# Layer 1 of a two-layer network: results, amplitudes, results, and the angles of an image further ahead

## The chip, the cores and the metric

The kernel runs on one NeuronCore of a Trainium2 chip. The metric is the device time of one execution in microseconds (us). The kernel before took 1475.18 us in the median of three runs (1472.35 to 1476.03).

## The reference

The input x has 16 images of 128 channels and 64 by 64 pixels, in float32. Two layers follow each other, and each adds its result to its input.

Layer 0 normalises x over groups of four channels and runs a diagonal LSTM over it: 127 sequential steps, each with a product of the gate weights and the states of the step before. Layer 1 treats every pixel on its own. It is this part that the change touches:

```python
xq = xf @ pre_w.T + pre_b            # 128 channels -> 4 angles a pixel
z = _simulate(xq, q_weights)         # 4 qubits, 16 complex amplitudes, 4 expectations
out = z @ post_w.T + post_b          # 4 -> 128 channels
x = x + out                          # xf is the group-normalised x
```

`_simulate` is linear in products of the sines and cosines of the angles, so the kernel writes it as sine of sums of angles, a fixed matrix that gives the amplitudes, their squares, and a matrix that leads from the squares to the 128 output channels.

## The kernel before

Layer 0 runs as one long loop of steps over all images at once, with its result kept in the on-chip buffer `ring`, which holds 40 of the 64 rows of every image. The lower 24 rows are written to a scratch tensor `low` in device memory, and layer 1 loads them back. Statistics of layer 0's result close that part, and `b_image` (L730) is the last value that layer 1 waits for.

Layer 1 then goes image by image. An image is 4096 pixels, taken as eight tiles of 128 channels by 512 pixels: tiles 0 to 2 come from `low`, tiles 3 to 7 lie in `ring`. For image b there are these stages:

- `load(b)`: three DMAs of 256 KB on GpSimd's queue (POOL, L749) fetch tiles 0 to 2 into buffers of the pool `lowp`.
- `angles(b)`: eight matmuls (16 passes in the profile, L760) write the angles of all pixels of the image into one PSUM tile `theta`. The same function then makes the sines: ScalarE adds the image's bias (L770), VectorE takes off the nearest whole turn with two instructions (L771, L772), ScalarE takes the sine (L773). The result `y` is kept in `turns`.
- `squares(b)`: two matmuls (L780) give the amplitudes `am`, and ScalarE squares each (L782) into a tile `sq`.
- `outputs(b, h)` for the halves h = 0 and 1: four matmuls (L789) give four PSUM tiles `po`, 512 pixels each.
- `finish(b, h, po)`: VectorE adds each `po`, the output bias and the input tile in place (L806). SyncE's queue (SP) writes the result out: in half 0 the three low tiles of 256 KB each (L808) and one piece of `ring` of 256 KB, in half 1 one piece of 1 MB (both L811).

All of this stands under a hand-written order (`manual_schedule`): each engine runs its instructions in the order in which the source issues them. Before the loop come the loads of images 0 to 2, `angles(0)`, `angles(1)` and `squares(0)`. Round b of the loop is then: `load(b+3)`, `outputs(b,0)`, `finish(b,0)`, `angles(b+2)`, `outputs(b,1)`, `squares(b+1)`, `finish(b,1)`.

The pool `lowp` has 11 buffers, two more than the nine of three images. A load into a buffer waits until the result of the tile that was in it has been written out. So in round b the first two tiles of image b+3 take buffers of image b-1, and its third takes the buffer of tile 0 of image b, whose writing out is issued in that same round. The tiles `po` have one buffer each, so that `outputs(b,1)` follows the evictions of `finish(b,0)` tile by tile. The pool `trp` holds two buffers each of `y` and of the two `sq`.

Of the kernel before, what the change touches and what calls it, by code (L numbers as in the profile page):

```python
# [11 lines left out]
F32 = mybir.dt.float32  # L12
# [4 lines left out]
P = 128  # L17
NB = 16
# [8 lines left out]
CHUNK = 2 * BLOCK  # L27
# [51 lines left out]
def kernel(  # L79
# [50 lines left out]
    def block(r):  # L130

        return (r + AHEAD if r < SLOTS else r - SLOTS) // ROWS
# [600 lines left out]

    lowp = ctx.enter_context(tc.tile_pool(name="lowp", bufs=11))
    trp = ctx.enter_context(tc.tile_pool(name="trp", bufs=2))
    ps_t = ctx.enter_context(tc.tile_pool(name="ps_t", bufs=2, space=PSUM))
    ps_a = ctx.enter_context(tc.tile_pool(name="ps_a", bufs=1, space=PSUM))
    ps_o = ctx.enter_context(tc.tile_pool(name="ps_o", bufs=1, space=PSUM))  # L740
    NT = NLOW * NW // CHUNK
    x1s, turns, sqs = {}, {}, {}

    def load(b):

        x1s[b] = []
        for k in range(NT):
            lt = lowp.tile([P, CHUNK], F32, name=f"low{b}_{k}", tag="low")
            nc.gpsimd.dma_start(out=lt, in_=low[b, :, k * CHUNK : (k + 1) * CHUNK])  # L749
            x1s[b].append(lt)  # L750
        for r in range(NLOW, NH, 2 * ROWS):
            q = block(r)
            x1s[b].append(ring[:, q : q + 2, b, :])

    def angles(b):
        th = ps_t.tile([P, CHUNK], F32, name=f"theta{b}", tag="theta")
        for h in range(2):

            for j in (2, 3, 1, 0):
                nc.tensor.matmul(  # L760
                    th[32 * j : 32 * j + 32, :],
                    lhsT=w_image[:, b, 16 - 16 * h : 48 - 16 * h],
                    rhs=x1s[b][2 * j + h],
                    start=(h == 0),
                    stop=(h == 1),
                    tile_position=(0, 32 * j),
                )

        y = trp.tile([P, CHUNK], F32, name=f"y{b}", tag="y")
        nc.scalar.activation(y, th, AF.Identity, bias=b_image[:, b : b + 1])  # L770
        nc.vector.tensor_scalar(th, y, ROUND, ROUND, ALU.add, ALU.subtract)  # L771
        nc.vector.tensor_sub(y, y, th)  # L772
        nc.scalar.activation(y, y, AF.Sin, scale=TWO_PI)  # L773
        turns[b] = y

    def squares(b):
        sqs[b] = []
        for h in range(2):
            am = ps_a.tile([P, CHUNK], F32, name=f"am{b}_{h}", tag=f"am{h}")
            nc.tensor.matmul(am, lhsT=w_amp[:, h, :], rhs=turns[b], start=True, stop=True)  # L780
            s = trp.tile([P, CHUNK], F32, name=f"sq{b}_{h}", tag=f"sq{h}")
            nc.scalar.activation(s, am, AF.Square)  # L782
            sqs[b].append(s)

    def outputs(b, h):
        po = [ps_o.tile([P, CHUNK], F32, name=f"po{b}_{h}_{j}", tag=f"po{j}") for j in range(4)]
        for j in range(4):
            k = 32 * j
            nc.tensor.matmul(  # L789
                po[j],  # L790
                lhsT=w_out[k : k + 32, :],
                rhs=sqs[b][h][k : k + 32, :],
                start=True,
                stop=True,
                tile_position=(k, 0),
            )
        return po

    def finish(b, h, po):
        for j in range(4):  # L800
            k = 4 * h + j
            x1 = x1s[b][k]
            y = po[j]
            if k >= NT:
                y = y.rearrange("p (k n) -> p k n", n=BLOCK)
            nc.vector.scalar_tensor_tensor(x1, y, b_out, x1, ALU.add, ALU.add)  # L806
            if k < NT:
                nc.sync.dma_start(out=ov[b, :, k * CHUNK : (k + 1) * CHUNK], in_=x1)  # L808
        for r0, r1 in (((NLOW, SLOTS),), ((SLOTS, NH),))[h]:
            q = block(r0)  # L810
            nc.sync.dma_start(  # L811
                out=ov[b, :, r0 * NW : r1 * NW].rearrange("c (k n) -> c k n", n=BLOCK),
                in_=ring[:, q : q + (r1 - r0) // ROWS, b, :],
            )

    with tc.manual_schedule():
        for b in range(3):
            load(b)
        angles(0)
        angles(1)  # L820
        squares(0)
        for b in range(NB):
            if b + 3 < NB:
                load(b + 3)
            po = outputs(b, 0)
            finish(b, 0, po)
            if b + 2 < NB:
                angles(b + 2)
            po = outputs(b, 1)
            if b + 1 < NB:  # L830
                squares(b + 1)
            finish(b, 1, po)


# [35 lines left out]
```

## Time and profile before

| What | Value |
|---|---|
| median of three runs | 1475.18 us |
| profiled execution, own time | 1472.09 us |
| its span | 1470.3 us |
| layer 1: from b_image (1310.63) to the end of the span | 159.7 us |
| busy in the whole span | PE 1368.3, VectorE 975.4, GpSimd 890.1, ScalarE 765.4 us |
| moved by DMA in the whole span | 106.99 MB |

Times within the profile count from the start of the span. PE is TensorE, DVE is VectorE, ACT is ScalarE, POOL is GpSimd, SP is SyncE. PEclk is the granted clock of TensorE as a share of its full speed. The shares of the whole span are averages over two unlike layers: in layer 0, which is most of the time, TensorE is busy nearly throughout and DMA is nearly idle; in layer 1, the last tenth, DMA is busy nearly throughout.

### The profile page before, as it was taken

To read this page: it belongs to the slowest core of one execution; us is meant where nothing else is said; L and a number is where in the kernel's file an instruction comes from. 1 tells how busy PE (TensorE), PEld (TensorE's weight loads), DVE (VectorE), ACT (ScalarE), POOL (GpSimd) and SP (SyncE) were. 2 spreads that over 40 slices of the span, in tenths; PEclk is the share of its full clock that TensorE was granted. 3 is DMA by queue.
4 is the path that set the end of the run, shared out by engine and by line. 5 is a ranking of instruction groups with operands and counts; after the bars stand their busy time and mean duration, and the time that the engine had idled before them with its cause. 6 is when DMAs were issued, how large, how long until landed. Compare 5 with 4: busy or idle time off the path is not lost. (4 is left out here: it accounts for less than half of the span.)

```text
span 1470.3 us, 19434 instructions
## 1 busy us (share of the span) xinstructions
PE 1368.3 (93%) x5798; PEld 970.2 (66%) x5798; DVE 975.4 (66%) x2458; ACT 765.4 (52%) x1862; POOL 890.1 (61%) x1694
## 2 busy tenths in 40 slices
PE   4658999999999999999999999999999999859987
PEld 3658887777667767676677677767776787832322
DVE  6974566566765667877767775555555678767765
ACT  3545666565555555555555555555555665422221
POOL 1125787766667767788788767666766776521110
PEclk9999999999999999999999999999999999979987
DMA  9970000000000000134433000000000000028987
GB/s 311 375 254 1 2 1 1 1 1 1 1 0 1 1 0 1 58 128 138 135 118 112 1 1 0 1 1 1 0 1 1 1 1 1 1 79 303 327 281 269
DMA packets 86192, 106.99 MB, mean 73 GB/s; under 512 B 4024, under 2 KB 70728, under 8 KB 86088
## 3 DMA queue, kind: packets, MB, share of 16 engines
q1 hardware_dynamic: 80576, 92.29, 18.4%
q0 software_dynamic: 3840, 12.59, 2.7%
q8 instruction: 46, 0.75, 0.2%
q10 hardware_dynamic: 1672, 0.89, 0.2%
q14 instruction: 58, 0.48, 0.1%
HBM read 59.61 MB, written 46.14 MB: 72 GB/s over the span
## 5 line engine op out<-in xcount | busy, mean ns | idle before, releaser
L491 PE MATMUL ps<-xn,wxT 128*128 128x512 f32 (+18 forms) x1280 | 480.7, 518 | 2.0 <-POOL xn L483 2.0
L604 DVE TENSOR_TENSOR ps<-ps,both 128x256 f32<-128x256 f32 (+9 forms) x544 | 219.7, 408 | 325.7 <-PE ps L582 320.2
L608 ACT ACTIVATE ps<-ps,bias 128x512 f32<-128x512 f32 (+23 forms) x480 | 268.5, 581 | 252.5 <-DVE ps L604 213.0
L491 PEld LDWEIGHTS ps<-xn,wxT 128*128 128x128 f32 x1280 | 231.8, 191 | 174.5 <-issue 155.5
L633 ACT COPY both<-ps 128x256 f32<-128x256 f32 (+9 forms) x544 | 191.7, 355 | 178.5 <-PE ps L582 158.9
L582 PE MATMUL ps<-diff,w1T 128*128 128x256 f32 (+14 forms) x1088 | 283.7, 363 | 0.0
L582 PE MATMUL ps<-diff,w0T 128*128 128x256 f32 (+14 forms) x1088 | 283.2, 362 | 0.0
L524 POOL TENSOR_TENSOR ring<-ring,hst 128x256 f32<-128x256 f32 (+8 forms) x488 | 247.5, 539 | 24.7 <-DVE hst L672 24.7
L582 PEld LDWEIGHTS ps<-hst,wsT 128*128 128x128 f32 x1088 | 195.9, 190 | 85.5 <-DVE hst L672 35.4
L582 PE MATMUL ps<-hst,wsT 128*128 128x256 f32 (+14 forms) x1088 | 241.3, 365 | 5.7 <-DVE hst L672 4.3
L582 PEld LDWEIGHTS ps<-diff,w0T 128*128 128x128 f32 x1088 | 199.7, 190 | 21.2
L582 PEld LDWEIGHTS ps<-diff,w1T 128*128 128x128 f32 x1088 | 199.2, 190 | 20.8
L483 POOL TENSOR_TENSOR xn<-xn,rstd 128x512 f32<-128x512 f32 (+10 forms) x160 | 170.7, 1067 | 15.2 <-DVE rstd L152 2.7
L478 POOL TENSOR_TENSOR xn<-ring 128x256 f32<-128x256 f32 (+8 forms) x213 | 147.4, 702 | 0.0
L672 DVE TENSOR_TENSOR hst<-g,ps 128x256 f32<-128x256 f32 (+13 forms) x320 | 108.4, 369 | 44.9 <-ACT g L663 41.7
L663 ACT ACTIVATE g<-cst 128x256 f32<-128x256 f32 (+20 forms) x320 | 103.0, 368 | 64.1 <-DVE cst L662 63.6
L473 POOL TENSOR_TENSOR xn<-ring,mean 128x16 f32<-128x16 f32 (+8 forms) x247 | 130.7, 539 | 3.6 <-DVE mean L138 2.6
L515 POOL TENSOR_TENSOR diff<-hst 128x240 f32<-128x240 f32 (+9 forms) x136 | 103.0, 758 | 39.0 <-DVE hst L672 35.7
L662 DVE TENSOR_TENSOR cst<-cst,ps 128x256 f32<-128x256 f32 (+20 forms) x320 | 104.6, 368 | 5.5
L659 DVE TENSOR_TENSOR ps<-ps,g 128x512 f32<-128x512 f32 (+20 forms) x160 | 95.1, 594 | 18.6 <-ACT g L608 17.6
L685 POOL COPY edge<-hst 128x16 f32<-128x16 f32 x64 | 25.1, 392 | 135.9 <-DVE hst L672 135.9
L652 DVE TENSOR_TENSOR cst<-cst,ps 128x512 f32<-128x512 f32 (+20 forms) x160 | 92.8, 580 | 16.9 <-ACT ps L608 9.4
(149 smaller groups left out, 1219.9 us busy)
## 6 DMA issues: line engine op xcount, KB each, us to landing
ring<-in_x_dram SPq DMA_DIRECT2D x16, 1024.0 KB, 7.5
out_dram<-ring SPq DMA_DIRECT2D x16, 1024.0 KB, 5.9
rest<-in_x_dram SPq DMA_DIRECT2D x48, 256.0 KB, 5.0
low<-ring SPq DMA_DIRECT2D x6, 2048.0 KB, 7.5
ring<-in_x_dram SPq DMA_DIRECT2D x6, 2048.0 KB, 8.4
low<-low POOLq DMA_DIRECT2D x48, 256.0 KB, 4.0
out_dram<-low SPq DMA_DIRECT2D x48, 256.0 KB, 6.1
ring<-in_x_dram SPq DMA_DIRECT2D x16, 256.0 KB, 7.8
```

The source lines that it names most:

```text
L473: nc.gpsimd.tensor_sub(by_pairs(xn, 0, j, n), x0, over(mean1, n))
L478: nc.gpsimd.tensor_sub(by_pairs(xn, 1, j, n), lower, of)
L483: nc.gpsimd.tensor_mul(v, v, r)
L491: nc.tensor.matmul(ps[g][:, :, a:b], lhsT=wxT[:, g * 128 : (g + 1) * 128], rhs=xns[t % 2][:, :, a:b], start=True, stop=True,)
L515: nc.gpsimd.tensor_sub(diff[:, 0, a1:b], now[:, 1, a1 - NB : b - NB], now[:, 0, a1:b])
L524: nc.gpsimd.tensor_add(x1, x1, by_pairs(new, q, j, n))
L582: nc.tensor.matmul(out, lhsT=w[:, g * 128 : (g + 1) * 128], rhs=rhs, start=False, stop=True, skip_group_check=True,)
L604: nc.vector.tensor_add(v, v, both[g][:, a:b])
L608: nc.scalar.activation(to[:, :, a:w], ps[g][:, :, a:w], FUNC[g], bias=bias[:, g : g + 1])
L633: nc.scalar.copy(both[g][:, a:b], ps[g][:, 0, a:b])
L662: nc.vector.tensor_add(c[:, q], c[:, q], ig[:, q])
L672: nc.vector.tensor_mul(new[:, q, a:v], th[:, q, a:v], act[GO][:, q, a:v])
```

## The change

The stages stay the same, with the same matmuls, the same instructions on VectorE and ScalarE and the same DMAs. What changes is their order and their buffers.

`angles` keeps only the matmuls. A new function `sines` holds the four instructions that followed them; it is a generator that stops before the sine, so that the caller can place the two parts apart. Loads run four images ahead (12 buffers), the matmuls of the angles three images ahead at the end of a round, and the sines two images ahead in the middle of it. Round b is now: `load(b+4)`, `outputs(b,0)`, `finish(b,0)`, the first three instructions of `sines(b+2)`, `squares(b+1)`, the sine of image b+2, `outputs(b,1)`, `finish(b,1)`, `angles(b+3)`. Round 0 is an exception: it takes the angles and the sines of image 2 after its results, and then the angles of image 3. The second square is written over `y`, which has three buffers; the first has two.

```diff
-    lowp = ctx.enter_context(tc.tile_pool(name="lowp", bufs=11))
-    trp = ctx.enter_context(tc.tile_pool(name="trp", bufs=2))
+    lowp = ctx.enter_context(tc.tile_pool(name="lowp", bufs=12))
+    sinp = ctx.enter_context(tc.tile_pool(name="sinp", bufs=3))
+    sqp = ctx.enter_context(tc.tile_pool(name="sqp", bufs=2))
...
-
-        y = trp.tile([P, CHUNK], F32, name=f"y{b}", tag="y")
+        ths[b] = th
+
+    def sines(b):
+
+        th = ths[b]
+        y = sinp.tile([P, CHUNK], F32, name=f"y{b}", tag="y")
         nc.scalar.activation(y, th, AF.Identity, bias=b_image[:, b : b + 1])
         nc.vector.tensor_scalar(th, y, ROUND, ROUND, ALU.add, ALU.subtract)
         nc.vector.tensor_sub(y, y, th)
+        turns[b] = y
+        yield
         nc.scalar.activation(y, y, AF.Sin, scale=TWO_PI)
-        turns[b] = y
 
     def squares(b):
-        sqs[b] = []
+        ams = []
         for h in range(2):
             am = ps_a.tile([P, CHUNK], F32, name=f"am{b}_{h}", tag=f"am{h}")
             nc.tensor.matmul(am, lhsT=w_amp[:, h, :], rhs=turns[b], start=True, stop=True)
-            s = trp.tile([P, CHUNK], F32, name=f"sq{b}_{h}", tag=f"sq{h}")
+            ams.append(am)
+
+        sqs[b] = [sqp.tile([P, CHUNK], F32, name=f"sq{b}", tag="sq"), turns[b]]
+        for am, s in zip(ams, sqs[b]):
             nc.scalar.activation(s, am, AF.Square)
-            sqs[b].append(s)
...
     with tc.manual_schedule():
-        for b in range(3):
+        for b in range(4):
             load(b)
         angles(0)
+        for _ in sines(0):
+            pass
         angles(1)
+        later = sines(1)
+        next(later)
         squares(0)
+        next(later, None)
         for b in range(NB):
-            if b + 3 < NB:
-                load(b + 3)
+            if b + 4 < NB:
+                load(b + 4)
             po = outputs(b, 0)
+            later = sines(b + 2) if 0 < b < NB - 2 else iter(())
             finish(b, 0, po)
-            if b + 2 < NB:
-                angles(b + 2)
-            po = outputs(b, 1)
+            next(later, None)
             if b + 1 < NB:
                 squares(b + 1)
+            next(later, None)
+            po = outputs(b, 1)
             finish(b, 1, po)
+            if b == 0:
+                angles(2)
+                for _ in sines(2):
+                    pass
+            if b + 3 < NB:
+                angles(b + 3)
```

More of the change, by code (lines that the diff above doesn't have):

```diff
@@ L741 @@
     NT = NLOW * NW // CHUNK
-    x1s, turns, sqs = {}, {}, {}
+    x1s, ths, turns, sqs = {}, {}, {}, {}
     def load(b):
```

## The prediction, made before the result was known

> **What bounds the kernel now.** I first read the slices of the whole span (40 slices of 36.8 us), to see where layer 1 differs from layer 0.
>
> ```profile
> PE   4658999999999999999999999999999999859987
> DVE  6974566566765667877767775555555678767765
> DMA  9970000000000000134433000000000000028987
> ```
>
> TensorE carries layer 0; in the last four slices DMA comes up to 9. The change touches only those. Next, windows of layer 1; the columns are the window, its length, busy PE, PEld, DVE, ACT and POOL, the granted clock, the DMA share and GB/s.
>
> ```profile
> 1340.00:1360.00 20.00, 18.23 (x88) 5.73 (x92) 13.30 (x20) 4.83 (x9) 3.22 (x6) 1.00 0.97 333
> 1360.00:1380.00 20.00, 18.91 (x84) 5.96 (x76) 15.52 (x24) 5.82 (x11) 3.22 (x6) 1.00 0.96 334
> 1400.00:1420.00 20.00, 15.14 (x65) 4.05 (x63) 9.80 (x16) 3.17 (x5) 3.22 (x6) 0.83 0.77 257
> 1440.00:1471.00 31.00, 22.54 (x72) 7.54 (x72) 18.72 (x29) 3.93 (x7) 0.00 (x0) 0.76 0.72 245
> ```
>
> DMA is nearly full at times (333/0.97 to 334/0.96: about 345 GB/s) and far from it at others. What leaves it idle is in the chain that ended last (start, length, what). This is one turn of it, from image 6 to image 8:
>
> ```profile
> 1373.23 0.71 DVE low L806
> 1373.95 6.74 DMA out_dram<-low
> ...
> 1381.24 3.23 DMA low<-low
> ...
> 1384.51 1.91 PE theta L760 x12
> 1386.42 1.07 PE po L789 x8
> 1387.49 1.07 PE am L780 x2
> ...
> 1388.61 2.50 DVE ring L806 x4
> ...
> 1391.29 0.71 DVE low L806
> ```
>
> A low tile is evicted, written out, its buffer reloaded, and the angles that need the reload hold up the outputs two rounds later. Last, where rounds begin on SP's queue:
>
> ```profile
> 1392.01 3.20 SPq L808 DMA_DIRECT2D out_dram<-low  x3
> ...
> 1400.20 3.00 SPq L808 DMA_DIRECT2D out_dram<-low  x3
> ...
> 1415.75 2.84 SPq L808 DMA_DIRECT2D out_dram<-low  x3
> ...
> 1423.70 2.55 SPq L808 DMA_DIRECT2D out_dram<-low  x3
> ```
>
> A round with its reload in time takes 7.95 us (1415.75 to 1423.70). One with a late reload takes more, once 15.55 us. All round starts: 1323.03, 1329.87, 1337.60 (rounds 0 to 2), 1442.13 (13), 1450.08 (14), 1460.29 (15); end 1470.3. Rounds 2 to 12 average (1442.13 - 1337.60)/11 = 9.50 us.
>
> **What the skill says.** The Trainium skill, page "DMA: Bandwidth & Descriptors", section Specifications, gives about 358 GB/s of device memory per core; my 345 fits. The same page, section "Queues, rings and completion order", says that each DMA engine takes the queues that have work in turn. The trace agrees: in 1340 to 1400 a reload of 256 KB took 2.8 to 7.4 us to land (median 5.1), beside the writing out. Page "TensorE: Matmul & The Clock Gate", section "What's actually happening", says that an idle window of some 3.4 us halves the clock. At 1406.53, after 4.86 us of waiting, a theta pass took 1.07 us and not 0.59, at a clock of 0.50; but the clock also fell at 1432 without such a wait[...]. Page "SBUF — State Buffer", section "Who interferes with whom", has VectorE and GpSimd share a port in some operations. The trace puts most of POOL's reload waits down to VectorE, but VectorE's evictions have one SBUF tensor, so I can't tell a lock from a coincidence; one instruction (0.74 us) bounds it, and the 0.55 us below contains the usual part.
>
> **The change, part by part.** No instruction is added or removed, so each part is a matter of place.
>
> *Angles at the end of a round, sines in its middle.* In a free round of before, VectorE waits 1.27 us for ACT's y, between finish(b,0) and the rounding of image b+2, because theta runs just ahead of it. That theta is now a round old, and the wait goes. What VectorE then has in a round: eight evictions at a pitch of (1422.93 - 1420.30)/4 = 0.66 us, 0.73 for L771 and 0.61 for L772, 6.6 us in all. PE: theta 1.9, am 2.0, po 2 x 1.1, 6.1 us. ACT: 0.69 + 0.63 + 2 x 0.6 = 2.5 us. So engines alone allow about 6.6 us a round instead of 7.95.
>
> *What DMA needs in a round:* 2.10 MB out and 0.79 MB in, 2.88 MB, at 345 GB/s 8.4 us. Engines of 7.95 or 6.6 us both outrun it; DMA or the loop through it decides.
>
> *The loop through the reload.* Before: from the eviction's start 0.77 us to the issue, 6.2 to landing (median in 1340 to 1400, 4.9 to 7.5), 0.55 to POOL's issue (1380.69 to 1381.24), 5.1 to landing, then from theta (1384.51) to the eviction (1391.29) 6.78: 19.4 us for two rounds, 9.7 each. The measured 9.50 confirms the sum. After: all three tiles of image b+4 take the buffers of image b, so the last waits for the third eviction, issued at 2.05 and not 0.77. Then 6.2 + 0.55 + 5.1 as before. But this theta stands ahead of po(b+2,0) and of nothing else: theta 1.91, po 1.14, and the eviction follows. 2.05 + 6.2 + 0.55 + 5.1 + 3.05 = 16.95 us for two rounds, 8.5 each. So the distance costs 1.3 us of a later reload and saves 3.7 us behind it. A late theta now holds po(b+2,0), am and everything behind them on PE; the sines of the image before and its evictions are already queued on VectorE and hide the first part. I take 8.5 us for rounds 2 to 12, since it is the largest of 6.6, 8.4 and 8.5. Bounds: with all landings longest (7.5 and 7.4) 20.55/2 = 10.3; with all shortest the loop gives 6.7, and DMA at 358 GB/s holds it to 8.05.
>
> *The start.* sq of image 0 stood behind the sine of image 1 on ACT and po began at 1321.03. Now it follows am directly: am begins at 1317.86, its first tile is done near 1318.9, sq takes 0.6, po begins near 1319.6: 1.4 us earlier. The 12th load goes out with the first 11, which end near 1306 and hide it; theta starts at 1310.9. Without that cover it would cost up to 3.4 us.
>
> *Rounds 0 and 1.* Round 0 has theta of two images behind po(0,1), before po(1,0): 2 x 1.9 us, of which the four evictions (2.7 us) hide a part. Counted from the first eviction at 1320.75: po(0,1) ends 1323.8, thetas 1327.6, po(1,0) 1328.7, so 7.9 us; before 6.84. Round 1: 7.0 by VectorE's 6.6 and the hand-overs; before 7.73.
>
> *Rounds 13 and 14.* No reload is left. Round 13: VectorE's 6.6 and what DMA has piled up, 7.2 (before 7.95). Round 14: before, am(15) stood behind po(14,1), and VectorE sat idle for 4.85 us waiting for po(15,0). Now am is ahead: 6.0 us at full clock; at half clock, where am took 3.78 and po 2.04, 0.6 + 3.78 + 2.04 + 2.7 = 9.1. I take 8.0 (before 10.21). Last round, unchanged: 10.0.
>
> *The other edits* (squares in place, buffer counts) cost nothing: y is read by both am passes before it is overwritten, three buffers of y cover the two images in work, and the square it feeds is needed a round later, under some 8 us of other work.
>
> Sum: 1321.6 + 7.9 + 7.0 + 11 x 8.5 + 7.2 + 8.0 + 10.0 = 1455.2 us of span, against 1470.3: 15.1 us less. The profiled execution's own time (1472.09) lies 1.8 us above its span, and the median of the runs 3.1 us above that; I take the difference off the median: 1475.2 - 15.1 = 1460.1 us.
>
> **Rivals.** *Reloads still late in part:* landing times lie between 4.9 and 7.5 and between 2.8 and 7.4, and a fuller DMA lengthens them; rounds of 9.1 give 11 x 0.6 = 6.6 us more, 1466.7. For it: the 6.47 us reload at 1400. Against it: the writing out is issued in order, so while a reload is on its way there is work behind it. *The distance is cancelled:* the later third tile eats what was saved, rounds stay at 9.5; the start and the end alone give -1.4 + 1.1 - 0.7 - 0.75 - 2.2 = -4.0, 1471.2. *Slower, by TensorE's clock:* PE's idle time now gathers at one place, ahead of theta. If that leaves the clock at 0.50, a round on PE is theta 3.62, am 3.78, po 2 x 1.8, 11.0 us: 11 x 1.5 = 16.5 more than before, less 4.0, 1487.7. The total is slower than before from 9.5 + 4.0/11 = 9.9 us a round, measurably from 10.3. Against it: 2.3 us of idle time in a round of 8.5 is short of the 4.86 us at 1406; for it: the drop at 1432. *Faster still:* DMA at 8.05 us a round and a full clock at the end, 1460 - 5 - 2 = 1453.
>
> **Chances.** The forecast 0.60, reloads still late 0.20, cancelled 0.10, slower 0.08, faster still 0.02. A change under 0.3% (4.4 us) can't be told from none with this kernel. Faster: 0.60 + 0.20 + 0.02 and a part of the cancelled, 0.84; within 0.3% 0.08; slower 0.08. The range 1453 to 1472 leaves out the slower case and a part of the cancelled one.
>
> **What would show it.** Right: round starts 8.3 to 8.7 us apart from round 2 to 12, none above 11; a DMA share of 0.97 or more there; VectorE's wait for y (39.5 us in all before) nearly gone; first issue on SP near 1321.6; VectorE's 4.85 us gap near the end shorter. Wrong: theta still waiting some us for low in most rounds with DMA share below 0.95 (loop longer than I sum), a clock of 0.5 in the middle of the layer, or a POOL queue that issues its reloads well over 0.6 us after the writing out has landed.

## The result, and the profile after

The changed kernel takes 1465.99 us in the median of 18 runs (1460.61 to 1470.85), the kernel before 1472.99 us in the 18 runs beside them. The ratio is 0.9952 with a 95% interval of 0.9939 to 0.9965: faster by 0.5%, 7.0 us, where 15.1 us were forecast.

The profiled execution of the changed kernel has a span of 1468.0 us. The slices of its whole span (36.7 us each) look like those of before, with layer 1 in the last four:

```profile
PE   4658999999999999999999999999999999858987
DVE  6883566566666666887777675555555687767775
DMA  9980000000000000133344000000000000028996
```

In this execution `b_image` was ready at 1314.20 us and in that of before at 1310.63. The change doesn't touch what stands ahead of it, and in the later runs it came between 1310.7 and 1314.8. So the two layers 1 are to be compared: 1468.0 - 1314.20 = 153.8 us after, 159.7 before, 5.9 us less. Windows of layer 1 after (window, length, busy PE, PEld, DVE, ACT, POOL, clock, DMA share, GB/s):

```profile
1340.00:1360.00 20.00, 16.61 (x75) 4.79 (x75) 13.40 (x21) 5.02 (x8) 3.21 (x6) 0.91 1.02 354
1360.00:1380.00 20.00, 18.91 (x87) 5.91 (x85) 18.64 (x30) 6.85 (x11) 3.21 (x6) 1.00 0.90 309
...
1420.00:1440.00 20.00, 16.77 (x71) 4.62 (x70) 11.64 (x19) 4.70 (x8) 1.61 (x3) 0.83 0.90 305
1440.00:1468.00 28.00, 19.47 (x48) 7.19 (x47) 17.08 (x26) 3.02 (x5) 0.00 (x0) 0.68 0.65 225
```

DMA is still not full throughout, and VectorE's busy time swings between 18.6 and 11.6 us in windows of one length: rounds of two kinds follow each other. SP's queue shows them where a round begins:

```profile
1340.15 3.28 SPq L817 DMA_DIRECT2D out_dram<-low  x3
...
1347.09 2.91 SPq L817 DMA_DIRECT2D out_dram<-low  x3
...
1360.13 1.65 SPq L817 DMA_DIRECT2D out_dram<-low  x3
...
1366.97 3.25 SPq L817 DMA_DIRECT2D out_dram<-low  x3
```

6.94, 13.04 and 6.84 us. The chain that ended last says what the long one waited for (start, length, what):

```profile
1339.39 0.74 DVE low L815
...
1340.15 6.04 DMA out_dram<-low
...
1346.74 0.18 POOL low L751
...
1347.40 0.15 POOL low L751
...
1348.04 6.57 DMA low<-low
...
1354.65 3.61 PE theta L762 x12
1358.26 1.07 PE po L798 x8
```

It is the loop of before (eviction, writing out, reload, theta, outputs), and it starts from the write of the first low tile. Behind it the three reloads are issued one after another, the last one takes 6.57 us to land, and theta's 12 passes take 3.61 us at a fallen clock (0.60 in 1354.0 to 1358.3). DMA is full at that time: between 1350 and 1360 it moves 352 to 383 GB/s at shares of 1.01 to 1.07. So it is full in bursts and has room between them. Last, who waited for whom over layer 1 (total us, times, longest):

```profile
DVE low L815 <- PE po L798: 28.4, 14, 6.3
...
PEld theta L762 <- DMA low<-low: 17.7, 7, 4.3
...
DVE theta L777 <- ACT y L776: 6.3, 3, 4.4
```

VectorE's wait for y fell from 39.5 us to 6.3, as the new order promises. In its place VectorE waits 28.4 us for `po`, ahead of which a late theta now stands; before, that was 7.2 us.

By step, from the starts of rounds on SP's queue:

| Step | before | forecast | after |
|---|---|---|---|
| b_image to the first write | 12.40 | 11.0 | 10.60 |
| round 0 | 6.84 | 7.9 | 8.51 |
| round 1 | 7.73 | 7.0 | 6.84 |
| rounds 2 to 12, sum | 104.53 | 93.5 | 100.33 |
| rounds 2 to 12, each | 9.50 | 8.5 | 9.12 |
| round 13 | 7.95 | 7.2 | 6.60 |
| round 14 | 10.21 | 8.0 | 10.21 |
| last round to the end | 10.01 | 10.0 | 10.71 |

Of the 9.2 us between the forecast and the measured difference in layer 1, 6.8 lie in rounds 2 to 12 and 2.2 in round 14.

### The profile page after: what moved, and what is told of

Same layout as the page of the kernel before. It is cut to its first block, busy times and chain, and to the rows that moved or that the text cites. A ratio compares the mean times of both kernels' runs of the same rounds, so it can differ in the third digit from the quotient of the medians.

```text
span 1468.0 us, 19391 instructions
## 1 busy us (share of the span) xinstructions
PE 1363.1 (93%) x5798; PEld 968.9 (66%) x5798; DVE 975.8 (66%) x2458; ACT 767.7 (52%) x1862; POOL 889.9 (61%) x1694
## 3 DMA queue, kind: packets, MB, share of 16 engines
q1 hardware_dynamic: 80576, 92.29, 18.6%
## 5 line engine op out<-in xcount | busy, mean ns | idle before, releaser
L659 DVE TENSOR_TENSOR ps<-ps,g 128x512 f32<-128x512 f32 (+20 forms) x160 | 95.2, 595 | 19.1 <-ACT g L608 17.8
```

## The experiments

The question was why a change that lets the engines run a round in 6.9 us brings them to 9.12 on average. The theory: the loop through the reload (eviction, writing out, reload, theta, outputs) still decides the late rounds, and the new order has used up the distance that the extra buffer gave. The rivals: DMA can't carry a round in less; the clock of TensorE makes the late rounds; the order of stages is what gained, and the distance did nothing.

All times below stand beside runs of the kernel before on the same chip, whose median moved between 1471.1 and 1473.0 us from group to group, so ratios are what to compare.

**Fifteen buffers.** The statistics tile moves to a pool that layer 0 gives back, which makes room for three more low tiles.

```diff
-    stats = const.tile([P, NB, NG2, 6], F32, name="stats")
+        stats_pool = scan.enter_context(tc.tile_pool(name="stats_pool", bufs=1))
+        stats = stats_pool.tile([P, NB, NG2, 6], F32, name="stats")
-    lowp = ctx.enter_context(tc.tile_pool(name="lowp", bufs=12))
+    lowp = ctx.enter_context(tc.tile_pool(name="lowp", bufs=15))
```

> The changed kernel with 15 buffers in lowp and not 12 (the statistics tile moves to a pool that layer 0 gives back, which makes the room). Image b+4 then takes the buffers of image b-1, free since the round before, so the reload has a round more. Theory (the loop through the reload sets every third round: 18 to 20 us for two rounds, with three reloads landing together and a half clock after the wait): theta no longer waits for low in rounds 2 to 12, they fall from 9.12 to 8.3 to 8.6 us on average, 6 to 9 us less than the changed kernel, a ratio to the kernel before of 0.989 to 0.991. Rival (DMA itself can't carry more than one round in 9.1 us, whoever waits for it): rounds stay at 9.0 to 9.2 and the ratio stays at 0.995, with the waits moved to other places.

Measured: 1450.77 us, a ratio of 0.9865 (0.9845 to 0.9885). Rounds 2 to 12 take 7.47 us on average, none over 8.2. The windows of layer 1:

```profile
1340.00:1360.00 20.00, 20.00 (x108) 6.82 (x108) 19.30 (x30) 7.54 (x12) 3.23 (x6) 1.00 0.99 348
1360.00:1380.00 20.00, 19.85 (x101) 6.15 (x100) 19.12 (x30) 6.84 (x11) 4.84 (x9) 1.00 1.04 382
1380.00:1400.00 20.00, 20.00 (x95) 6.56 (x92) 16.62 (x26) 6.56 (x11) 3.23 (x6) 1.00 1.06 383
```

The theory holds, and it was too modest. VectorE is busy 19.3 of 20 us, the clock stays at 1.00, and DMA moves 382 to 383 GB/s. So DMA was not at its limit with 333 GB/s and a share of 0.97: the 345 GB/s of the prediction, and the 8.4 us a round that follow from it, are refuted. Only rounds 7 to 11 (8.05 us on average, in which DMA moved 375 GB/s) look held by DMA. TensorE still waited for a reload once, for 0.8 us, between 1340 and 1422; in the changed kernel's layer 1 it was five times and 12.1 us. The step from b_image to the first write took 12.9 us here and not 10.6, because the first loads waited for the statistics, in whose place their pool lies: GpSimd stood idle ahead of the first load for 12.2 us, and for 0.4 us in the changed kernel.

**Ring tiles first.** In the changed kernel, theta's matmuls that need no reload come first.

```diff
-        for h in range(2):
-            for j in (2, 3, 1, 0):
+        order = ((2, 0), (3, 0), (2, 1), (3, 1), (1, 1), (0, 0), (0, 1), (1, 0))
+        for i, (j, h) in enumerate(order):
...
-                    start=(h == 0),
-                    stop=(h == 1),
+                start=(i == mine[0]),
+                stop=(i == mine[1]),
```

Here `mine` is the two places of the same j in the order.

> The changed kernel with the eight matmuls of theta in another order: the five that read ring first, then low 0, low 1 and low 2. After the last reload has landed one matmul (2 passes) is left and not 6 (12 passes). Theory (the loop through the reload decides): the loop of two rounds gets shorter by 10 passes of the 12, 1.2 us at full clock and up to 2.5 at half clock, so rounds 2 to 12 fall by 0.4 to 0.8 us on average, 4 to 9 us less than the changed kernel. Rival (DMA is the bound): no difference, within 2 us of the changed kernel.

Measured: 1462.27 us, ratio 0.9938 (0.9918 to 0.9958); rounds 2 to 12 average 8.69 us and not 9.12, a difference inside the expected one; the time is 3.7 us less by the medians and 2.1 by the ratios, under what was expected. The two intervals of the ratio overlap, so from the times alone the gain over the changed kernel is not certain; the trace supports it. The waits of this run for the reload, in which the changed kernel had 17.7 us, 7 times, 4.3 at the longest:

```profile
PEld theta L762 <- DMA low<-low: 16.3, 20, 1.3
```

The total is nearly the same, but it has broken up into waits of at most 1.3 us, and the clock stayed at 1.00 through 1320 to 1420.

**No large write.** The changed kernel without the 1 MB writes of half 1 of images 0 to 14.

```diff
+            if h == 0 or b == NB - 1:
                 nc.sync.dma_start(
                     out=ov[b, :, r0 * NW : r1 * NW].rearrange("c (k n) -> c k n", n=BLOCK),
```

> The changed kernel without the 1 MB write of half 1 of images 0 to 14 (the rows of ring from row 32 on are not written for them). DMA then has 1.83 MB a round and not 2.88. Theory (reload landings of 6.6 to 6.9 us come from sharing the DMA engines with the writes; engines alone need 6.6 to 6.9 us): landings fall below 5 us, no theta waits for low, all rounds take 6.8 to 7.1 us, rounds 2 to 12 take 75 to 78 us and not 100, and the clock stays at 1.00 to round 12. Rival (the clock or the engines make every third round late): rounds of 11 us and more remain.

Measured: 1438.74 us in a single run, whose output lacks those rows. Rounds 2 to 12 take 6.91 us each, all between 6.90 and 6.95. The reloads between 1340 and 1440 (the last number is the median time to landing), in the changed kernel and in this run, and a window of this run:

```profile
low<-low POOLq DMA_DIRECT2D x30, 256.0 KB, 5.5
```

```profile
low<-low POOLq DMA_DIRECT2D x30, 256.0 KB, 3.2
```

```profile
1360.00:1380.00 20.00, 20.00 (x108) 6.87 (x108) 19.30 (x30) 6.94 (x12) 4.83 (x9) 1.00 0.82 277
```

With the same buffers and the same order but less to share the DMA engines with, the reloads land in 3.2 us and not 5.5, none takes more than 4.9, and no theta waits. So in the new order neither the engines nor the clock make every third round late by themselves. The forecast of 6.6 us for the engines alone was 0.3 us short: between the last eviction of one image and the first of the next VectorE waits 0.20 us for `po`.

**The distance alone, in the old order, twice.** First the kernel before with loads four ahead and 14 buffers:

```diff
-        for b in range(3):
+        for b in range(4):
             load(b)
...
-            if b + 3 < NB:
-                load(b + 3)
+            if b + 4 < NB:
+                load(b + 4)
```

> The kernel before, order of stages unchanged, with loads four images ahead and 14 buffers (the statistics tile moved as in the run with 15). It is the distance of the reload alone. Theory (before, too, it was the loop through the reload that made 9.50 of 7.95): rounds 2 to 12 come to 8.4 to 8.7 us, 9 to 12 us less than the kernel before, a ratio of 0.992 to 0.994, as good as the changed kernel or better without its order. Rival (the order of angles, squares and results is what helped): rounds stay above 9.2, the ratio stays within 0.997 to 1.001.

Measured: 1461.78 us, ratio 0.994 (0.9921 to 0.9958), rounds 2 to 12 at 8.66 us. It pays the same delay at the start for its statistics tile: 14.7 us from b_image to the first write, 12.4 before. Between 1340 and 1440 theta waits for no reload at all. Still, five of the eleven rounds take 9.29 to 9.60 us and the others 7.95 or 7.96. In each of the five, theta's 16 passes take 3.3 to 3.5 us and not 1.92, at a clock of 0.53 to 0.56. Here are a slow and a full-speed theta of the chain, and a window over the slow one:

```profile
1341.31 3.48 PE theta L761 x16
...
1350.83 1.92 PE theta L761 x16
```

```profile
1341.30:1344.80 3.50, 3.50 (x21) 0.65 (x20) 1.47 (x3) 0.00 (x0) 0.07 (x1) 0.52 1.01 301
```

So the rival of the clock holds in the old order. With the reloads out of the way, a late round is one in which theta runs at a low clock: theta's excess, 1.3 to 1.6 us, is the excess of the round. What the 8.66 us have over 7.96 is not the loop through the reload. What makes the clock fall there stays open. TensorE was busy 2.90 of the 3.4 us ahead of this theta and 2.98 of the 3.4 us ahead of the one at 1350.83, which ran at full clock. Then the changed kernel's own 12 buffers and functions, with only the order of before:

```diff
             po = outputs(b, 0)
-            later = sines(b + 2) if 0 < b < NB - 2 else iter(())
             finish(b, 0, po)
-            next(later, None)
-            if b + 1 < NB:
-                squares(b + 1)
-            next(later, None)
+            if b + 2 < NB:
+                angles(b + 2)
+                for _ in sines(b + 2):
+                    pass
             po = outputs(b, 1)
+            if b + 1 < NB:
+                squares(b + 1)
             finish(b, 1, po)
...
-            if b + 3 < NB:
-                angles(b + 3)
```

> The changed kernel's buffers, loads four ahead and functions, but the order of stages of the kernel before (angles and whole sines of image b+2 between the two halves, squares after the second outputs, start as before). Of the change only the distance of the loads and the buffers are left. Theory (the order put theta of image b+4 into round b+1 and so used the extra distance up): here the loop through the reload spans three rounds, (14 to 15 + 6.8)/3 = 7.0 to 7.3 us each, and no longer binds; rounds 2 to 12 come to 8.0 to 8.7 us as in the run of the kernel before with loads four ahead, a ratio of 0.992 to 0.995, at least as fast as the changed kernel. Rival (the order of stages is what gains): rounds of 9.2 to 9.5 us, ratio 0.997 to 1.002.

Measured: 1461.09 us, ratio 0.9922 (0.9909 to 0.9935), rounds 2 to 12 at 8.56 us. With the changed kernel's buffers the order of before is faster than the changed order (0.9952, 0.9939 to 0.9965), and the intervals, though close, don't overlap. Six of the eleven rounds take 7.95 or 7.96 us. What ends such a round is the other chain, free of DMA (one round of it):

```profile
1364.98 1.93 PE theta L762 x16
...
1366.99 0.70 ACT y L776
...
1367.71 0.71 DVE theta L777
...
1368.44 0.70 DVE y L778
...
1369.16 0.63 ACT y L781
1369.79 0.50 ACT sq L792
...
1370.33 2.61 PE po L798 x8
```

1364.98 to 1372.94 is 7.96 us: theta, the four instructions of the sines, a square and the outputs one after another. This is the chain that the new order takes apart. Of the five longer rounds, two have a theta that reloads hold up, and three (9.26 to 9.65 us) a theta at a clock of 0.53 to 0.57. In the old order a reload issued for image b+4 is needed in the middle of round b+2; in the new one at the end of round b+1.

**Old and new order with enough buffers.** The old order again, with 15 buffers in two pools, of which only the second lies where the statistics were:

```diff
-    lowp = ctx.enter_context(tc.tile_pool(name="lowp", bufs=12))
+    lowpa = ctx.enter_context(tc.tile_pool(name="lowpa", bufs=8))
+    lowpb = ctx.enter_context(tc.tile_pool(name="lowpb", bufs=7))
```

> The order of stages of the kernel before with the changed kernel's functions, loads four ahead and 15 buffers in two pools of 8 and 7. It fills the fourth field beside the changed order with 12 and with 15 buffers and the old order with 12 (1461.1 us). Theory (once no reload is late, the engines' own chain decides: 7.95 us a round in the old order, 6.9 in the new one, and DMA about 8.05): every round takes 7.95 to 8.1 us, rounds 2 to 12 average 8.0 to 8.1 and not 8.56, the time is 1453 to 1457 us. The new order with 15 buffers without its early squares is then 4 to 7 us better, by the first rounds that run at 6.9 us. Rival (buffers are all): within 2 us of the changed order with 15 buffers.

Measured: 1458.31 us, 1.3 us above what was expected, ratio 0.99 (0.9873 to 0.9926). Rounds 2 to 12 average 8.11 us, as expected: all but one of them 7.95 or 7.96. The one of 9.65 has a theta at a clock of 0.53. So the order of stages is worth its place only when reloads are out of the way:

| Ratio to the kernel before | 12 buffers | 15 buffers |
|---|---|---|
| old order | 0.9922 | 0.9900 |
| new order | 0.9952 (the change) | 0.9865 |

The field below on the right still has the later start of its loads. The intervals of the two runs with 15 buffers overlap (0.9873 to 0.9926 and 0.9845 to 0.9885), so that the times alone leave the gain of the order, 7.5 us by the medians and 5.1 by the ratios, uncertain. The traces show where it lies: rounds 2 to 12 take 8.11 us in the one and 7.47 in the other.

**Fourteen buffers, new order.**

> The changed kernel with 14 buffers in two pools of 8 and 6. Of image b+4, two tiles take buffers of image b-1 and only the third that of image b, of its tile 0: as the kernel before has it, one round further. Theory (the sum of the loop: 0.77 + 6.2 + 0.55 + 5.1 to 6.6 + 3.05 = 15.7 to 17.2 us for two rounds): rounds 2 to 12 average 7.9 to 8.6 us, between 12 buffers (9.12) and 15 (7.5), the time is 1452 to 1459 us. Rival (only a reload that does not depend on the same image at all helps): rounds stay above 8.9 us, 1463 us or more.

Measured: 1457.09 us, ratio 0.9888 (0.986 to 0.9917), rounds 2 to 12 at 8.26 us. The average lies where the loop's sum puts it, but by luck: most rounds take 6.9 us and three take 13.6, 12.2 and 9.9, so that a late round and the one ahead of it make 20.5, 19.1 and 16.8 us and not 15.7 to 17.2, and more free rounds lie between them. With 12, 14 and 15 buffers the average goes 9.12, 8.26, 7.47.

**Squares of image 15 earlier.** One edit to the changed kernel:

```diff
-            if b + 1 < NB:
+            if b + 2 < NB:
                 squares(b + 1)
...
             finish(b, 1, po)
+            if b + 3 == NB:
+                squares(b + 2)
```

> The changed kernel with one edit: squares of image 15 at the end of round 13 and not in round 14. Theory (round 14 took 10.2 us because am at half clock, 3.7 us, stands between the two outputs): round 14 falls to 6 to 7.5 us, the time by 2.5 to 4 us, to a ratio of 0.992 to 0.993. Rival (the half clock makes po itself slow enough): round 14 stays above 9 us and the ratio at 0.995.

In the changed kernel, am of image 15 stood between the two outputs of image 14, at half clock, and VectorE waited behind it (timeline of the changed kernel):

```profile
1448.08 3.78 PE L787 MATMUL am<-y,w_amp 128*128 128x512 f32 x4
...
1451.79 2.05 PE L798 MATMUL po<-y,w_out 32*128 32x512 f32 x8
...
1453.87 2.73 DVE L815 SCALAR_TENSOR_TENSOR ring<-po,b_out,ring 128x512 f32<-128x512 f32 x4 [4.85 <-PE po L798]
```

Measured: 1462.52 us, ratio 0.9932 (0.9915 to 0.995). Round 14 fell from 10.21 to 5.26 us, round 13 rose from 6.60 to 7.84, 3.7 us less in both, and the time is 3.5 us less by the medians and 2.9 by the ratios; rounds 2 to 12 stayed at 9.13. Round 14 fell below the 6 to 7.5 us expected, and a part of its work moved to round 13. Again the intervals overlap, but the trace shows the gain at the place expected, and the two rounds together give its size.

**The kernel before, ring tiles first.**

> The kernel before with theta's matmuls ordered ring first, then low 0, low 1, low 2, as in the run of the changed kernel. In the kernel before the third tile is the one whose reload comes last from the same round, so after it one matmul of 2 passes is left and not 12 passes. Theory (in the kernel before, too, the reload's loop binds): two rounds get 1.2 us shorter where the reload is late, rounds 2 to 12 fall from 9.5 to 8.8 to 9.1 us, 4 to 8 us in all, ratio 0.994 to 0.997. Rival: within 0.2% of the kernel before.

Measured: 1468.42 us, ratio 0.9966 (0.9955 to 0.9977), 4.1 us less; rounds 2 to 12 at 8.88 us and not 9.50. So the kernel before was held by the reload too, in part.

**Together.** Fifteen buffers in two pools and the early squares, new order:

> The changed kernel with 15 buffers, in two pools of 8 and 7, so that only the last seven lie where the statistics were, and with squares of image 15 at the end of round 13 and not in round 14. Expected against the run with 15 buffers (1450.8 us): the first loads start after the end of layer 0's last step again and not after the statistics, 2 us less at the start; round 14 falls from 9.5 to 6.0 to 7.5 us, 2 to 3.5 us less. In all 4 to 5.5 us less, 1445 to 1447 us, a ratio of 0.982 to 0.984. Rival (DMA has the backlog to fill the end anyway): round 14 gets shorter but the end does not move, 1448 to 1449.

Measured: 1446.2 us, ratio 0.9821 (0.9805 to 0.9836), as expected, and better than both kernels. From b_image to the first write 10.9 us (12.9 with one pool); rounds 2 to 12 at 7.51; rounds 13 and 14 take 7.84 and 5.46 us.

## Why the prediction was right, and where its sizes were off

It forecast a faster kernel through a shorter loop, and so it is. Its range and its sign hold; its size, 15.1 us, was a little over twice the 7.0 measured. What came is its rival "reloads still late in part", to which it had given 0.20. That this rival's total, 1466.7 us, lies so near the 1465.99 measured is in part luck, since the kernel before ran 2.2 us faster beside it than in the three runs that the sum starts from. Of its signs, the wait for y and the start came as said. But four rounds took over 11 us where none should, the share of DMA was 0.97 or more in one of the five windows from 1340 to 1440, and the 4.85 us gap near the end stayed as it was.

*What bounds the kernel.* Right: the loop through eviction, writing out, reload and theta. Three edits show it from different sides: with 15 buffers TensorE's wait falls from 12.1 us to 0.8, without the large write it is gone, and with the ring tiles first it is shortened, in both kernels. For the kernel before it is not the whole: with loads four ahead no theta waits, and rounds of over 9 us remain, by the clock. So the 9.50 us that seemed to confirm the sum of 19.4 for two rounds hold a part that is not in that sum, such as the round of 10.47 us with the drop of the clock at 1432.

*Angles at the end of a round.* Right. VectorE's wait for y went from 39.5 to 6.3 us, and rounds without a late reload take 6.84 to 6.94 us against a sum of 6.6.

*The loop of two rounds, 16.95 us.* This is the step that failed. The turn in the chain above takes, from eviction to the end of po: 0.76 to the issue, 6.04 to landing, 0.55 to POOL's issue, 1.30 for the two reloads ahead, 6.57 to landing, 0.04, 3.61 for theta, 1.07: 19.9 us. The issue and the write together were priced about right (in this turn the second and third reload went out as fast as GpSimd issues them and did not wait for a later write, so 2.05 + 6.2 + 0.55 became 0.76 + 6.04 + 0.55 + 1.30). Two terms were too small. The last of three reloads that land together took 6.6 to 6.9 us in the four late turns of the chain, and I had put 5.1. That was misread: 5.1, like the range of 2.8 to 7.4, is taken over the reloads and the writes of low tiles together, and the reloads of that window alone have a median of 3.8 (18 of them, up to 6.9). The median of the reloads would have missed by more still. The loop waits for the last of three, so the upper end of the landing times was the number to take. And theta behind a wait ran at a lower clock: 3.61, 2.77, 1.91 and 3.63 us in the four late turns, where I had 1.91; that is 1.70 + 0.86 + 0 + 1.72 = 4.3 us of the 100.33. The clock's part is read from the trace; no run took it away alone. The rival's 9.1 us a round was not worked out from these terms, so that it agrees with the 9.12 measured says little.

*The average of the rounds.* I divided the loop by two. In fact a late round is followed by one or two that run at 6.9 us, with reloads already there, so loops of 18.2 to 21.7 us (19.8 on average) gave 9.1 a round and not 9.9. This error and the two terms above have opposite signs and cancel in part.

*DMA needs 8.4 us a round.* Wrong, as the run with 15 buffers shows at 7.47. I had taken a share of 0.97 for a full DMA. The figure of about 358 GB/s that the Trainium skill gives (page "DMA: Bandwidth & Descriptors", section Specifications) is no upper limit for this core either. Its row has it as the half of a stack that two cores share, and the run with 15 buffers moved 383 GB/s over 20 us. It did no harm here, since the loop's 8.5 lay above both.

*Start, rounds 0 and 1.* The start gained 1.8 us and not 1.4, round 0 lost 1.7 and not 1.1. Right in sum, since the two errors cancel.

*Round 14.* I took 8.0 between the bounds 6.0 and 9.1; it was 10.21, at half clock. am now stood between the two outputs of round 14, and VectorE's wait behind it was 4.85 us as before. It began 1.8 us after the first eviction of the round and not 0.6, since the last po of the first half ran at half clock as well; 1.8 + 3.7 + 2.0 + 2.7 = 10.2. The run with the early squares shows the place.

*The rival "slower, by TensorE's clock".* The clock did fall behind waits, to 0.50 in 1434.0 to 1437.7, but for single rounds. The skill's window of idle time (page "TensorE: Matmul & The Clock Gate", section "What's actually happening") fits them only roughly: after waits of 3.39, 2.18 and 2.41 us theta took 3.61, 2.77 and 3.63 us, and after one of 3.26 us it took 1.91. In the old order the clock fell to 0.53 with no wait of a matmul above 0.51 us in the 5 us ahead (theta at 1341.31 of the run with loads four ahead).

What stayed open: why a late round comes every third time, and what makes up the 6.6 us of the last landing. Without the large write the same three reloads go out together and none takes more than 4.9 us, so their sharing among themselves is not the whole. But that run also lets the 256 KB writes land sooner, so it does not tell the 1 MB write's part from theirs. That each DMA engine takes its queues in turn fits these landing times, but no run shows it by itself. The new order with loads three ahead was not run.

## What to carry to other kernels

Count the distance of a prefetch in time, from the event that frees its buffer to its first use and to what that use holds up, not in images. A reorder that moves the use from the middle of one round to the end of the round before spends what a further buffer bought: here the buffers alone gave 0.9922, buffers and order together 0.9952, and order with three more buffers 0.9865. Price a loop that waits for the last of several DMAs with the longest landing and not with the median, and don't take a busy share of 0.97 for the limit of DMA. When a wait is removed and long rounds remain, look at the clock before looking for more of the same wait. Before using a median of landing times, see which DMAs it is taken over.

## What the runs showed of the hardware that was not expected

- DMA moved 382 and 383 GB/s over two neighbouring windows of 20 us, at shares of 1.04 and 1.06 by the profile's count, with VectorE busy 19.1 and 16.6 us beside it. Windows with a share of 0.96 and 0.97 had moved 333 to 334.
- The clock of TensorE fell without any wait for a reload in the last rounds, where there is no theta: 0.68 in 1440 to 1468 of the changed kernel. It nearly doubled am, to 3.78 us from 1.98, and made it the work that VectorE waited for. In the old order with loads four ahead it fell to 0.53 to 0.56 during five thetas that waited for nothing, and each of those rounds took 1.3 to 1.6 us more.
